# A four-layer graph network on one core: one program per graph stage replaced by streams that a planner interleaves, with sorting networks per block and half of their values in PSUM

## The chip, the cores and the metric

The kernel runs on one core of a Trainium2 chip. The metric is the device time of one execution in microseconds (us). The kernel before takes 6,414.04 us, the median of three runs (6,408.74 to 6,424.81).

A core has five engines that each run their own queue of instructions in order: TensorE (PE, matrix products and transposes; PEld is its weight load), VectorE (DVE), ScalarE (ACT), GpSimd (POOL) and SyncE (SP, which here only issues DMAs). Engines wait for each other through semaphores. The on-chip memories are SBUF and PSUM, both 128 partitions wide; TensorE writes its results to PSUM.

## The reference: what is computed

There are 16 graphs of 1,024 nodes with 64 channels each, a dense weighted adjacency matrix per graph (some 16 neighbours a node), and four pre-layernorm residual layers. Cut to what matters:

```python
h = relu(layernorm(x)); x = x + tanh([h, adj@h] @ W1 + b1) @ W2 + b2              # layer 0
h = relu(layernorm(x)); x = x + ((adj + I) @ h) / rowsum(adj + I)                 # layer 1
h = relu(layernorm(x)); x = x + mlp(h + quantiles(h over kept neighbours)) * mask # layer 2
h = relu(layernorm(x)); x = x + (adj @ h / colsum(adj)) @ Wn + h @ Ws + bias      # layer 3
```

Layer 2 is the irregular one. A node with more than 10 neighbours loses some of them, in both directions ("dilation": every `skip`-th by rank, `skip` from the count). For every node and channel the values of the kept neighbours are sorted, and the quantiles at 0.25, 0.5 and 0.75 are summed with the weights 0.25, 0.5, 0.25:

```python
sv = sort(where(valid, x_of_neighbour, big), axis=neighbours)
for tau, wt in zip((.25, .5, .75), (.25, .5, .25)):
    pos = tau * (m - 1); lo, hi = floor(pos), ceil(pos)
    agg += wt * (sv[lo] * (1 - (pos - lo)) + sv[hi] * (pos - lo))
```

## The kernel before

All work of interest is in `direct_path`. (`general_path` is a slower way that is run after it only where a node's neighbour count lies outside what the direct path provides for; with these inputs it is not run.) A graph's 1,024 nodes are 8 blocks of 128 partitions. A loop over `b` (at the end of the function) treats graph `b` up to its gathers, and in the same pass the sorting of graph `b-1`. The work of one graph is:

1. `load_graph` (L834): loads 8 row blocks of the adjacency, turns each with TensorE (L847), copies it back by ScalarE (L848) into `adjt`, writes the 0/1 neighbour mask `nb` on VectorE (L850, L852), counts neighbours, spills the turned matrix to DRAM (`adjt_d`, for layer 3), and sums degrees.
2. `dilated` (L869): ranks of neighbours by prefix matmuls (L892, L895), ScalarE's `Abs` (L899) and a compare on VectorE (`gone`, L900); then the kept neighbours as keys and their counts (L906 to L917).
3. `layer0` (L1052); then `order` (L923), which sorts the nodes by their kept count: `pos` is each node's place in that order (L938).
4. `neighbour_lists` (L941): the keys are scattered into sorted order through DRAM with 8 indirect DMAs (L946), loaded back block by block, and the neighbour numbers of each node are read out 8 at a time with VectorE's MAX8 (L960) and MATCH_REPLACE (L963). The indices of all blocks are made in one instruction (`index`, behind L967), then the quantile weights (L972 to L992).
5. `layer1` (L1066), the layernorm for layer 2 (`preln`, L791 on, with a memset on GpSimd, L806), and the store of its result `h_d` to DRAM (L1144).
6. Gathers and sorting: since the nodes are sorted by count, block 0 needs room for up to 38 neighbours and the last ones for 13. `GROUPS` lists (first block, blocks, most, least) for five groups. For each group, `aggregate` of the graph before runs on VectorE: a Batcher sorting network of `max` and `min` over whole 64-channel rows (L1031) that moves each value between two SBUF buffers (`raw`, `other`), the weights (L1044), a reduce (L1047), a store (L1048). Then `gather` (L1007) fetches this graph's neighbours: one indirect DMA of 128 rows by 64 channels for each block and place, 152 a graph, issued by GpSimd.
7. `layer2` (L1087) for the graph before: 8 indirect DMAs bring the sorted-order result back to node order (`res`, L1090), an add (L1092), transposes (L814), an MLP; then `layer3` (L1106), which reloads `adjt_d`, and the store of the output.

Order: the tile framework keeps each engine's instructions in about the order of the program text and inserts the waits. So on GpSimd's one queue lie, for each pass of the loop, the 8 scatters of graph `b`, its 152 gathers, and behind these the 8 read-backs of graph `b-1`. On TensorE's queue the transposes of `layer2` (L814) of graph `b-1`, which wait for those read-backs, lie ahead of the transposes of the adjacency (L847) of graph `b+1`. Each `raw` buffer exists once (`raws`, `bufs=1`), so a group's gathers of graph `b` follow its sorting of graph `b-1`.

Of the kernel before, what the change touches and what calls it, by code (L numbers as in the profile page):

```python
# [17 lines left out]
P = 128  # L18
# [14 lines left out]

GROUPS = [(0, 1, 38, 17), (1, 1, 20, 15), (2, 2, 18, 12), (4, 2, 16, 10), (6, 2, 13, 1)]
KW = N + 2

E_ID, E_ONE, E_CAP, E_LOW, E_CN, E_Q, E_END = 0, 128, 256, 264, 272, 280, 320
# [3 lines left out]
def _span(cap, low):  # L43

    return (low - 1) // 4, -(-3 * (cap - 1) // 4)


def _network(cap, low):


    n = 1
    while n < cap:
        n *= 2
    layers, a = [], 1
    while a < n:
        layers.append([(i, i + a) for i in range(n - a) if i // a % 2 == 0])
        a *= 2
    a, e = n // 4, 1
    while a > 0:
        d = e  # L60
        while d > 0:
            layers.append([(i, i + d * a) for i in range(a, n - d * a) if i // a % 2 == 1])
            d //= 2
        a, e = a // 2, 2 * e + 1
    lo, hi = _span(cap, low)
    live, kept = set(range(lo, hi + 1)), []
    for layer in reversed(layers):
        layer = [(i, j, i in live, j in live) for i, j in layer if j < cap and (i in live or j in live)]
        for i, j, _, _ in layer:
            live |= {i, j}  # L70
        if layer:
            kept.append(layer)
    return kept[::-1]


def _patterns(items):


    left, out = set(items), []
    while left:  # L80
        best = None
        for x in sorted(left):
            steps = sorted({(y[2] - x[2], y[3] - x[3]) for y in left if y[:2] == x[:2] and y > x})

            def run(start, v):
                row = [start]
                while (z := (*x[:2], row[-1][2] + v[0], row[-1][3] + v[1])) in left:
                    row.append(z)
                return row

            for v in [None, *steps]:
                row = [x] if v is None else run(x, v)
                if best is None or len(row) > len(best[0]):
                    best = (row, x, [(len(row), *(v or (0, 0)))])
                for w in steps if v else []:
                    cover, m = list(row), 1
                    while all((z := (*x[:2], r[2] + m * w[0], r[3] + m * w[1])) in left and z not in cover
                              for r in row):
                        cover += [(*x[:2], r[2] + m * w[0], r[3] + m * w[1]) for r in row]
                        m += 1  # L100
                    if m > 1 and len(cover) > len(best[0]):
                        best = (cover, x, [(m, *w), (len(row), *v)])
        left -= set(best[0])
        out.append(best[1:])
# [3 lines left out]
def _program(cap, low):  # L108


    home, out = [0] * cap, []
    for layer in _network(cap, low):
        for greater in (True, False):
            items = [(home[i], home[j], i, j) for i, j, a, b in layer if (a if greater else b)]
            out += [(greater, p) for p in _patterns(items)]
        for i, j, _, _ in layer:
            home[i] ^= 1
            home[j] ^= 1
    lo, hi = _span(cap, low)
    return out, _patterns([(home[q], 0, q, q - lo) for q in range(lo, hi + 1)])  # L120


QT = sum((_span(cap, low)[1] + 1 - _span(cap, low)[0]) * n for _, n, cap, low in GROUPS)
# [582 lines left out]

@with_exitstack
def direct_path(ctx: ExitStack, tc: tile.TileContext, t: dict, out: bass.AP, flag):


# [6 lines left out]
    loads = ctx.enter_context(tc.tile_pool(name="loads", bufs=2))  # L717
    graph = ctx.enter_context(tc.tile_pool(name="graph", bufs=1))
    nodes = ctx.enter_context(tc.tile_pool(name="nodes", bufs=2))
    lists = ctx.enter_context(tc.tile_pool(name="lists", bufs=2))  # L720
    work = ctx.enter_context(tc.tile_pool(name="work", bufs=2))
    raws = ctx.enter_context(tc.tile_pool(name="raws", bufs=1))
    psum = ctx.enter_context(tc.tile_pool(name="psum", bufs=1, space=bass.MemoryType.PSUM))
    dram = ctx.enter_context(tc.tile_pool(name="dram", bufs=2, space=bass.MemoryType.DRAM))

    def bank(dt=F32):
        return psum.tile([P, 2048 // mybir.dt.size(dt)], dt, tag="t", name="pt", bufs=4)

    def bank2():
        return psum.tile([P, N], F32, tag="t2", name="pt2", bufs=2)  # L730

    def big(shape, dt=F32):

        return work.tile(shape, dt, tag="big", name="big", bufs=3)

    def mid(shape, dt=F32):

        return work.tile(shape, dt, tag="mid", name="mid", bufs=4)

    tt, ts, act = nc.vector.tensor_tensor, nc.vector.tensor_scalar, nc.scalar.activation  # L740

# [15 lines left out]
    nc.vector.memset(bad, 0.0)  # L757

# [10 lines left out]
    def along(name, src):  # L769
        w = const.tile([P, C], F32, name=name)  # L770
        nc.gpsimd.dma_start(w, bass.AP(tensor=src.tensor, offset=src.offset, ap=[[0, P], [1, C]]))
        return w[:, None, :].to_broadcast([P, NB, C])

    w01, w02 = weight("L0_gnn_W1", 2 * C), weight("L0_gnn_W2", C)
    b01, b02 = column("L0_gnn_b1", C), along("b02", t["L0_gnn_b2"])
    w21, w22 = weight("L2_gnn_W1", C), weight("L2_gnn_W2", P)
    b21, b22 = column("L2_gnn_b1", P), along("b22", t["L2_gnn_b2"])
    w3n, w3s = weight("L3_gnn_W_neighbors", C), weight("L3_gnn_W_self", C)
    b3 = along("b3", t["L3_gnn_bias"])
# [5 lines left out]
    pm = bank()  # L785
    nc.tensor.transpose(pm[:, :B * NB], maskf, identf[:B * NB, :B * NB])
    mask = const.tile([P, B, NB], F32, name="mask")
    nc.vector.tensor_copy(mask.rearrange("p b i -> p (b i)"), pm[:, :B * NB])


    def preln(x):  # L791

        ha = nodes.tile([P, NB, C + 1], F32, name="ha", bufs=3)
        s = nodes.tile([P, 4, NB], F32, name="stat")
        xc = mid([P, NB, C])
        sq = mid([P, NB, C])
        nc.vector.tensor_reduce(s[:, 0], x, AX.X, ALU.add)
        ts(s[:, 1], s[:, 0], 1.0 / C, None, op0=ALU.mult)
        tt(xc, x, s[:, 1, :, None].to_broadcast([P, NB, C]), ALU.subtract)
        act(sq, xc, AF.Square)  # L800
        nc.vector.tensor_reduce(s[:, 2], sq, AX.X, ALU.add)
        act(s[:, 3], s[:, 2], AF.Sqrt, bias=eps, scale=1.0 / C)
        nc.vector.reciprocal(s[:, 2], s[:, 3])
        tt(xc, xc, s[:, 2, :, None].to_broadcast([P, NB, C]), ALU.mult)
        act(ha[:, :, :C], xc, AF.Relu)
        nc.gpsimd.memset(ha[:, :, C:], 1.0)  # L806
        return ha

    def transposed(h, dst):

        for q in range(2):
            p = bank()
            for u in range(4):
                nc.tensor.transpose(p[:C, u * P:(u + 1) * P], h[:, 4 * q + u, :C], identf)  # L814
            nc.scalar.copy(dst[:, q * 512:(q + 1) * 512], p[:C, :])  # L815

    def messages(h, rows_of, dst, p0, n=C):

        p = bank2()
        for j in range(NB):  # L820
            a = rows_of(j)
            for q in range(2):
                s = slice(q * 512, (q + 1) * 512)
                nc.tensor.matmul(p[p0:p0 + n, s], h[:, j, :n], a[:, s], start=j == 0, stop=j == NB - 1)  # L824
        nc.scalar.copy(dst, p[p0:p0 + n, :])

    def per_node(p, lhs, w):

        for i in range(NB):
            nc.tensor.matmul(p[:, i * C:(i + 1) * C], lhs[:, i * P:(i + 1) * P], w, start=True, stop=True)  # L830
# [3 lines left out]
    def load_graph(b):  # L834


        adjt = graph.tile([P, NB, N], F32, name="adjt")
        nb = graph.tile([P, NB, KW], F16, name="nb")
        mn = nodes.tile([P, NB], F32, name="mn")
        for i in range(NB):  # L840
            a = loads.tile([P, N], F32, name="a")
            nc.sync.dma_start(a, adj[b, i * P:(i + 1) * P, :])
            for q in range(2):
                p = bank()
                for u in range(4):
                    j = 4 * q + u
                    nc.tensor.transpose(p[:, u * P:(u + 1) * P], a[:, j * P:(j + 1) * P], identf)  # L847
                nc.scalar.copy(adjt[:, 4 * q:4 * q + 4, i * P:(i + 1) * P],  # L848
                               p.rearrange("p (u m) -> p u m", m=P))
            ts(nb[:, i, :N], a, 0.0, None, op0=ALU.is_gt)  # L850
            d = slice(i * P, (i + 1) * P)
            tt(nb[:, i, d], nb[:, i, d], offdiag, ALU.mult)  # L852
            sink = lists.tile([P, N], F16, name="sink", bufs=1)
            act(sink, nb[:, i, :N], AF.Copy, accum_out=mn[:, i:i + 1])
        adjt_d = dram.tile([NB, P, N], F32, name="adjt_d")
        deg = nodes.tile([P, 3, NB], F32, name="deg")
        for j in range(NB):
            nc.sync.dma_start(adjt_d[j], adjt[:, j])
            sink = lists.tile([P, N], F16, name="sink", bufs=1)
            act(sink, adjt[:, j], AF.Copy, accum_out=deg[:, 0, j:j + 1])  # L860
# [414 lines left out]
```

## Time and profile before

| what | value |
|---|---|
| median of three runs | 6,414.04 us (6,408.74 to 6,424.81) |
| span of the profiled execution | 6,913.4 us (7.8% above the median) |
| granted TensorE clock, mean | 0.625 |
| VectorE busy | 3,475.0 us, 50%, 8,634 instructions |
| GpSimd busy | 2,968.2 us, 43%, 2,770 instructions |
| TensorE busy | 2,119.5 us, 31%, 9,027 matmuls |
| ScalarE busy | 1,383.5 us, 20%, 2,178 instructions |
| gathers, L1007 | 2,432; 2,635.4 us, 1,084 ns each; 1,581.4 us of idle before them |
| sorting networks, L1031 (the two largest groups of the page) | 1,488 of 528 ns and 1,424 of 485 ns |
| longest kind of wait | TensorE at L814 for VectorE's L1092: 2,687.6 us in 16 waits |
| DMA | 372.80 MB, mean 54 GB/s |

How to read it: the page describes one execution under the hardware profiler. Its span is from the first instruction to the last and is the time to which durations of the page belong; the median is from runs without it. "Busy" is the share of the span in which an engine executes an instruction, and says nothing of what it waits for. A group's line gives how many, their total, the mean duration of one in ns, and the idle time of the engine just before them with what ended it. The rows of digits cut the span in 40 slices; each digit is the busy share of a slice in tenths.

### The profile page before, as it was taken

Reading aid. Unit: us, or ns where it says so; the run is one execution under the profiler, and the core shown is the slowest. Engines: PE = TensorE matmul, PEld = TensorE weight load, DVE = VectorE, ACT = ScalarE, POOL = GpSimd, SP = SyncE. Lnnn points to the kernel's source line nnn. Section 1 sums busy time; section 2 is a strip of 40 time slices with the busy share of each in tenths; the row PEclk is TensorE's granted clock in tenths of the full one; section 3 lists DMA queues with packets and bytes.
Section 4 is the critical chain, followed back from the end, with each engine's and each line's share of the span. In section 5 each row is a group of like instructions: output and inputs, shape, how many; then the busy total and the mean of one; then the engine's idle time right before and its main releaser. Section 6 shows DMA issues by size and latency. Waiting matters only on the chain.

```text
span 6913.4 us, 34033 instructions
## 1 busy us (share of the span) xinstructions
PE 2119.5 (31%) x9027; PEld 1036.5 (15%) x9027; DVE 3475.0 (50%) x8634; ACT 1383.5 (20%) x2178; POOL 2968.2 (43%) x2770
## 2 busy tenths in 40 slices
PE   6230251402624035140261404504046400624003
PEld 3010121201311012120130102202022100312001
DVE  3247371663715637066370655607556471833826
ACT  5110141300412013030141202203023300403000
POOL 0626417164071631716417172270722746153460
PEclk8565575755856557575585656757567655856556
DMA  3311213112241131312323123131233221232211
GB/s 116 53 24 25 61 65 67 51 23 57 89 76 26 24 70 61 56 57 24 69 95 59 29 21 87 57 47 57 21 87 95 37 36 23 87 67 49 37 21 49
DMA packets 234412, 372.80 MB, mean 54 GB/s; under 512 B 119104, under 2 KB 119296, under 8 KB 234208
## 3 DMA queue, kind: packets, MB, share of 16 engines
q0 software_dynamic: 92608, 117.94, 13.9%
q1 hardware_dynamic: 141456, 251.93, 11.0%
q8 instruction: 73, 1.20, 0.1%
q14 instruction: 131, 1.07, 0.1%
q10 hardware_dynamic: 144, 0.66, 0.0%
HBM read 257.00 MB, written 113.31 MB: 54 GB/s over the span
## 4 chain that ended last, share of the span: by engine, by line
issue 27%; DVE 17%; POOL 17%; another core or an unknown queue 13%; PE 13%; DMA 8%; ACT 3%; POOLq 0%; DVEq 0%; SPq 0%; ACTq 0%
POOL raw L1007 15%; PE pt L824 5%; DVE found L960 4%; DVE other L1031 3%; DVE raw L1031 3%; DVE rest L963 3%; DMA keys_d<-nb,pos 3%; DMA at<-adjt_d 3%; POOL keys_d L946 1%; DMA a<-in_adj_dram 1%; PE pt L830 1%; PE pt L895 1%; PE pt L847 1%; DMA raw<-h_d,index 1%
## 5 line engine op out<-in xcount | busy, mean ns | idle before, releaser
L1007 POOL DMA_INDIRECT raw<-h_d,index x2432 | 2635.4, 1084 | 1581.4 <-issue 732.0
L1031 DVE TENSOR_TENSOR other<-raw 128x128 f32<-128x128 f32 (+8 forms) x1488 | 759.8, 528 | 356.4 <-DMA raw<-h_d,index 287.5
L814 PE MATMUL pt<-ef,res 128*64 128x128 f32 x128 | 30.6, 420 | 2687.6 <-DVE res L1092 2687.6
L1031 DVE TENSOR_TENSOR raw<-other 128x256 f32<-128x256 f32 (+10 forms) x1424 | 669.1, 485 | 10.5 <-issue 3.5
L806 POOL MEMSET ha<- 128x8 f32 x64 | 8.6, 144 | 1444.5 <-PE pt L824 1402.5
L824 PE MATMUL pt<-adjt,ha 128*65 128x512 f32 (+1 forms) x1024 | 480.4, 630 | 231.5 <-issue 209.1
L1092 DVE TENSOR_TENSOR res<-res,ha 128x512 f32<-128x512 f32 x16 | 11.1, 691 | 1058.0 <-DMA res<-agg_d,pos 1058.0
L946 POOL DMA_INDIRECT keys_d<-nb,pos x128 | 194.4, 1519 | 687.9 <-DVE pos L938 431.8
L847 PE MATMUL pt<-ef,a 128*128 128x128 f32 x1024 | 234.5, 407 | 685.4 <-DMA a<-in_adj_dram 462.7
L815 ACT COPY big<-pt 64x512 f32<-64x512 f32 x96 | 55.3, 578 | 1877.2 <-PE pt L814 1460.1
L814 PEld LDWEIGHTS pt<-ef,res 128*64 128x64 f32 x128 | 19.9, 168 | 2694.0 <-DVE res L1092 2603.2
L895 PE MATMUL pt<-eh,nbt 128*128 128x512 f16 (+3 forms) x1536 | 339.9, 361 | 186.4 <-issue 122.0
L850 DVE TENSOR_SCALAR nb<-a 128x1024 f16<-128x1024 f32 x128 | 89.2, 697 | 481.5 <-DMA a<-in_adj_dram 339.4
L848 ACT COPY adjt<-pt 128x512 f32<-128x512 f32 x256 | 147.6, 585 | 826.0 <-remote 613.5
L900 DVE TENSOR_SCALAR gone<-ab,sf 128x1024 f16<-128x1024 f16 x128 | 61.5, 481 | 496.8 <-issue 258.1
L847 PEld LDWEIGHTS pt<-ef,a 128*128 128x128 f32 x1024 | 192.0, 214 | 727.2 <-issue 600.4
L824 PE MATMUL pt<-at,ha 128*64 128x512 f32 x512 | 264.1, 647 | 83.0 <-DMA at<-adjt_d 82.7
L960 DVE MAX8 found<-rest 128x8 f16<-128x1024 f16 x224 | 270.4, 1216 | 0.5
L899 ACT ACTIVATE ab<-pt,sf 128x1024 f16<-128x1024 f32 x128 | 142.8, 1116 | 512.4 <-remote 328.1
L895 PEld LDWEIGHTS <-nbt 128*128 128x128 f16 x1536 | 156.5, 106 | 508.5 <-issue 246.6
L824 PEld LDWEIGHTS pt<-adjt,ha 128*65 128x65 f32 (+1 forms) x1024 | 146.5, 146 | 550.4 <-issue 531.3
L1031 DVE TENSOR_TENSOR other<-raw,other 128x256 f32<-128x256 f32 (+4 forms) x592 | 205.1, 348 | 33.2 <-remote 24.5
(138 smaller groups left out, 4763.3 us busy)
## 6 DMA issues: line engine op xcount, KB each, us to landing
a<-in_adj_dram SPq DMA_DIRECT2D x128, 512.0 KB
adjt_d<-adjt SPq DMA_DIRECT2D x128, 512.0 KB
at<-adjt_d SPq DMA_DIRECT2D x128, 512.0 KB
raw<-h_d,index POOLq DMA_INDIRECT x2432
k<-keys_d SPq DMA_DIRECT2D x128, 256.5 KB
x<-in_x_dram SPq DMA_DIRECT2D x16, 256.0 KB
h_d<-ha SPq DMA_DIRECT2D x16, 256.0 KB
out_dram<-x SPq DMA_DIRECT2D x16, 256.0 KB
```

Source lines behind the costliest of these rows:

```text
L824: nc.tensor.matmul(p[p0:p0 + n, s], h[:, j, :n], a[:, s], start=j == 0, stop=j == NB - 1)
L830: nc.tensor.matmul(p[:, i * C:(i + 1) * C], lhs[:, i * P:(i + 1) * P], w, start=True, stop=True)
L847: nc.tensor.transpose(p[:, u * P:(u + 1) * P], a[:, j * P:(j + 1) * P], identf)
L848: nc.scalar.copy(adjt[:, 4 * q:4 * q + 4, i * P:(i + 1) * P], p.rearrange("p (u m) -> p u m", m=P))
L850: ts(nb[:, i, :N], a, 0.0, None, op0=ALU.is_gt)
L895: nc.tensor.matmul(p[:, o:q * 512 + 512], nbt[:, j, :], stair[:, o - j * P:q * 512 + 512 - j * P], start=False, stop=j == 4 * q + 3)
L899: act(ab, p, AF.Abs, bias=sf[:, 2, i:i + 1], scale=2.0)
L946: nc.gpsimd.indirect_dma_start(keys_d, bass.IndirectOffsetOnAxis(ap=pos[:, i:i + 1], axis=0), nb[:, i, :], None)
L960: nc.vector.max(out=e, in_=src)
L963: nc.vector.match_replace(out=rest, in_to_replace=e, in_values=src, imm_value=0.0)
L1007: nc.gpsimd.indirect_dma_start(raw[:, s, i * C:(i + 1) * C], None, h_d, bass.IndirectOffsetOnAxis(ap=index[:, at:at + 1], axis=0))
L1031: tt(o, a, b, ALU.max if greater else ALU.min)
```

## The change

It rewrites `direct_path`; the general path and the host side stay, but for tables.

- **Order.** The loop over graphs is gone. The work of a graph is some fifteen generators ("streams"): `tail` (layers 2 and 3), `load_a`, `load_x`, two of `turn` (transposes), `masks`, two of `ranks`, two of `keyed`, `ordered`, `fetched`, `listed`, `weighted`, `layers01`, `spill`, `gathered`, `sorted_`. Each yields operations with an engine, a cost in us, and the regions that they read and write. A planner, when the program is built, takes again and again the operation that can start first, and among those that can start within 0.02 us the one of the lowest rank: `10*b` and a small number for preparation and tail of graph `b`, `10*b+1000` for its gathers and networks. That fixes each engine's order; the framework's own scheduling is turned off. Buffers are allocated once and streams wait in the planner until one is free; PSUM is three pairs of banks for matmuls and one pair (`places`, 16 slots of 64 channels) for the networks.
- **Blocks.** Each of the 8 blocks has a network of its own, with the caps and least counts `CAPS` and `LOWS`: 132 gathers a graph, where there were 152. Only the places that some quantile needs are kept (`_needed`). Five `raw` buffers serve the 8 blocks: blocks 5, 6 and 7 use those of blocks 1, 2 and 3. The index is written block by block.
- **Networks.** Of the values that a layer of the network writes, one side goes to PSUM and one to SBUF as the table `SIDES` says; `_boxes` joins operations with up to three strides. Instructions of the networks: 5,248 before, 6,384 after.
- **To ScalarE and TensorE.** Layernorm's centering and squares are 8 ScalarE instructions with an accumulator, its scaling 8 more with bias and scale; column sums of the adjacency come from the accumulator of the copies behind the transposes; biases and residual adds become matmuls; the weighted places are summed by matmuls with the identity (1,120 in all) where VectorE reduced them; aggregates are stored by block (128 DMAs for 80).

The core of the diff; the new functions that it calls, `_boxes` and `_program` (the list of a network's operations and where each value lies), follow from the description above:

```diff
-GROUPS = [(0, 1, 38, 17), (1, 1, 20, 15), (2, 2, 18, 12), (4, 2, 16, 10), (6, 2, 13, 1)]
+CAPS = (33, 19, 17, 15, 14, 13, 11, 10)
+LOWS = (19, 17, 15, 14, 13, 11, 10, 3)
+PLACES = 16
...
+class _Planner:
+    def start(self, op):
+        t = self.free.get(op.engine, 0.0)
+        for aps, writes in ((op.ins, False), (op.outs, True)):
+            for name, lo, hi in aps:
+                for a, b, end, wrote, engine in self.used.get(name, ()):
+                    if a < hi and lo < b and (writes or wrote):
+                        if engine != op.engine:
+                            end += 0.12 + (0.4 if op.engine == "DVE" and wrote else 0.0)
+                        t = max(t, end)
+        return t
...
+    def run(self):
...
+            heads = {}
+            for s in self.streams:
+                if s[3] is not None:
+                    heads.setdefault(s[3].engine, []).append((self.start(s[3]), s))
+            best = None
+            for these in heads.values():
+                first = min(t for t, _ in these)
+                t, s = min(((t, s) for t, s in these if t <= first + 0.02), key=lambda c: (c[1][0], c[1][1]))
+                if best is None or t < best[0]:
+                    best = (t, s)
...
+            self.commit(op, t)
...
-    def aggregate(g, raw, wts, agg_d):
...
-            tt(o, a, b, ALU.max if greater else ALU.min)
...
-        nc.vector.tensor_reduce(agg, part.rearrange("p q w -> p w q"), AX.X, ALU.add)
...
+    def tt(o, a, b, op):
+        return _Op("DVE", 0.068 + n_of(o) / 960, lambda: nc.vector.tensor_tensor(o, a, b, op), [o], [a, b])
...
+    def gather(o, src, at):
+        return _Op("POOL", 1.25, lambda: nc.gpsimd.indirect_dma_start(
+            o, None, src, bass.IndirectOffsetOnAxis(ap=at, axis=0)), [o], [src, at], 1.8)
...
+    def preln(x, h, s):
...
+        for i in range(NB):
+            yield act(junk, x[:, i], AF.Square, bias=s[:, 1, i:i + 1], accum=s[:, 2, i:i + 1])
+        yield act(s[:, 3], s[:, 2], AF.Sqrt, bias=eps, scale=1.0 / C, table="sqrt")
...
+        for i in range(NB):
+            yield act(h[:, i, :C], x[:, i], AF.Relu, bias=s[:, 4, i:i + 1], scale=s[:, 2, i:i + 1])
...
+    def listed(b):
...
+            yield ts(index[:, c], found[:, c], -1.0, ALU.mult, float(N), ALU.add)
+            post(("index", b, k))
...
+    def gathered(b):
+        yield "wait", ("h", b)
+        index, h_d = indexes[b % 2], h_ds[b % 3]
+        for k in range(NB):
+            yield "wait", ("index", b, k)
+            before = [(c, i) for c in (b - 1, b) for i in range(NB) if home[i] == home[k] and (c, i) < (b, k)]
+            if before and before[-1][0] >= 0:
+                yield "wait", ("block", *before[-1])
+            raw = raws[home[k]]
+            for s in range(CAPS[k]):
+                at = LOFF[k] + s
+                yield gather(raw[:, s, :], h_d, index[:, at:at + 1])
+            post(("raw", b, k))
...
+    def sorted_(b):
...
+                mem = (raws[home[k]], other, places)
...
+                yield tt(o, a, c, ALU.max if kind == "max" else ALU.min)
...
+            def issue(p=p, n=n):
+                for q in range(n):
+                    nc.tensor.matmul(p, identf, part[:, q, :], start=q == 0, stop=q == n - 1)
+            yield pe(0.12 * n, issue, [p], [part[:, :n]])
+            yield copy(aggs[:, k], p)
...
+            yield dma(agg_ds[b % 2][k * P:(k + 1) * P], aggs[:, k])
...
-    for b in range(B + 1):
...
+    for b in range(B):
+        plan.add(10 * b, tail(b))
...
+        plan.add(10 * b + 2, ordered(b))
+        plan.add(10 * b + 4, listed(b))
+        plan.add(10 * b + 3, layers01(b))
...
+        plan.add(10 * b + 1000, gathered(b))
+        plan.add(10 * b + 1000, sorted_(b))
+    with tc.manual_schedule():
+        plan.run()
```

## The prediction

> **What bounds the kernel now.** I read the page's first two sections, then the chain, then the waits, then the timeline of one graph's gathers.
>
> ```profile
> span 6913.4 us, 34033 instructions
> DVE  3247371663715637066370655607556471833826
> POOL 0626417164071631716417172270722746153460
> issue 27%; DVE 17%; POOL 17%; another core or an unknown queue 13%; PE 13%; DMA 8%; ACT 3%; POOLq 0%; DVEq 0%; SPq 0%; ACTq 0%
> L1007 POOL DMA_INDIRECT raw<-h_d,index x2432 | 2635.4, 1084 | 1581.4 <-issue 732.0
> ```
>
> No engine bounds it: DVE is busy 50%, POOL 43%, TensorE 31%, and the rows of tenths swing with a period of two to three slices, one graph. The chain hands from engine to engine. First gather at 193 us, end of the last at 6,707: (6,707−193)/16 = 407 us a graph. Its 152 gathers take 152×(1.084+0.305 gap, from the "issue" wait) = 211 us; for 196 us POOL gathers nothing. Why the next graph's preparation does not run beside the gathers, the waits tell (us in total, times, longest):
>
> ```profile
> PE pt L814 <- DVE res L1092: 2687.6, 16, 310.2
> ACT big L815 <- PE pt L814: 1460.1, 50, 234.4
> POOL raw L1007 <- DVE s L972: 519.4, 10, 53.1
> POOL keys_d L946 <- DVE pos L938: 431.8, 15, 102.4
> ```
>
> TensorE stands 168 us a graph in front of the transposes of layer 2, which need the result read back through POOL's queue, behind all 152 gathers; the next graph's TensorE work is queued behind them. POOL then waits for that preparation.
>
> **The change part by part.** All costs are in the profiled execution's time; it is 6,913/6,414 = 1.078 of the median (range of the runs 6,409 to 6,425).
>
> *Gathers and POOL.* 152 gathers a graph become 132: indirect DMAs 16×(132+8 scatters+8 read-backs) = 2,368 for 2,688. An undisturbed one and its gap, from the timeline:
>
> ```profile
> 3140.83 9.22 POOL L1007 DMA_INDIRECT raw<-h_d,index  x1 [0.31 <-issue]
> 3149.13 2.71 DVE L1047 TENSOR_REDUCE agg<-part 128x128 f32<-128x1536 f32 x1
> 3150.35 0.94 POOL L1007 DMA_INDIRECT raw<-h_d,index  x1 [0.30 <-issue]
> ```
>
> 0.944+0.305 = 1.249 us; 2,368× = 2,958 us. The 9.22 is a gather held while DVE ran networks; it ends 0.92 after the reduce began. I set all gathers against what DVE ran: 1,860 with idle DVE mean 0.943; 360 begun under two-SBUF-input network operations 1.706 (+0.76); 28 under the compare of L850 1.787 (+0.84); 26 under the reduce 0.944. After, of 3,600 us or so, DVE does such two-SBUF work for 381 us (1,600 operations; the other 5,664 have an input in PSUM) and compares for 128 us: 10.6% of 2,368 is 251×0.76 = 191 us, 3.6% is 84×0.84 = 71. MAX8 and MATCH_REPLACE (631 us) never met a gather: bounds 0 (like the reduce) and 17.5%×2,368×0.84 = 350; I take 0, being one-input like the reduce, and keep 350. Head: the index is written per block, so gathers need not wait for a graph's whole lists (668/16 = 42 us) and start at about 193−42+4 = 155; tail from the last read-back (6,844.6 to the end 6,913, 69) about 75. POOL's side: 2,958+191+71+155+75 = 3,450.
>
> The Trainium skill, "SBUF — State Buffer", section "Who interferes with whom", says a DVE instruction with at most one SBUF input outside the two-port modes leaves GpSimd alone, and one with two SBUF inputs contends only with SBUF reads. The trace agrees with 0.944 under the reduce and 1.706 under two inputs. By that rule the operations with an input in PSUM cost nothing, as taken.
>
> The smaller caps hold these inputs exactly (their largest and smallest kept counts, block by block, are the new lists), so the general path stays unrun.
>
> *DVE.* Start to start, an SBUF tensor_tensor costs 0.068+n/960 (n elements a row). By that: networks 5,248 operations, 1,852 us, become 6,384, 1,590 (smaller caps; one block at a time and three places for a value, so more and smaller ones); weights 168→98; the sum over kept places 115→0 (to TensorE, 1,120 identity matmuls, about 0.3 each from L830's 0.276: 336 us); lists 668→631; layernorms 160→60 and layer adds 134→56 (to ScalarE's bias and accumulate forms and to bias matmuls). Sum of all instructions: 3,352→2,677.
>
> But dependence costs. An operation that needs the one just before it starts later:
>
> ```profile
> 3476.62 1.21 DVE L1031 TENSOR_TENSOR other<-raw 128x1024 f32<-128x1024 f32 x1
> 3477.86 1.23 DVE L1031 TENSOR_TENSOR raw<-other 128x1024 f32<-128x1024 f32 x1
> 3479.00 0.48 DVE L900 TENSOR_SCALAR gone<-ab,sf 128x1024 f16<-128x1024 f16 x1
> ```
>
> The dependent one starts 1.24 after its predecessor, the independent one 1.14: over 219 pairs 0.116 more. The before program has 420 immediate dependences of 8,412; the after 5,036 of 9,038, for it plans one block's network at a time: 584 us for 49. DVE's occupied time: 2,677+584 = 3,261 for 3,401. With 115 idle at the head and the tail's 75: 3,451.
>
> Writes to PSUM (3,088) are not in the trace of before. Reads are, at no cost: 687 ns against 683 for the same shape:
>
> ```profile
> L1064 DVE TENSOR_TENSOR x<-x,pt 128x512 f32<-128x512 f32 x16 | 11.0, 687 | 206.4 <-PE pt L830 191.2 <-remote 15.2
> L799 DVE TENSOR_TENSOR mid<-x,stat 128x512 f32<-128x512 f32 x64 | 43.6, 683 | 0.3
> ```
>
> Bounds −0.068 (the fixed part vanishes: −210 us) to +0.116 each (+358); I take 0, by the read. The Trainium skill, "Perfetto Trace Analysis", section "Optimizing Scalar/DVE Operations", puts DVE's overhead at about 60 ns on SBUF and 125 on PSUM; an estimate by it, 65 ns on 5,664, adds 368 us of engine time. The reads of this trace (4 ns) do not show it.
>
> *ScalarE, TensorE, SP.* 512 squares and 512 Relus of 64 elements, 256 accumulator reads (0.2 each), copies: from 1,384 to some 1,730 us; TensorE 2,120 plus 336 and 124 for bias and residual matmuls, 2,580. Both lie beside POOL and DVE with over 800 us of idle left; without that cover, 350 and 460. SP issues 694 DMAs for 646 (aggregates by block, 128 for 80), waits apart a few us, hidden too.
>
> *Order and waits.* Build-time list scheduling puts read-backs and scatters between gathers (about two gathers, 2.5 us, from one to the next) and the next graph's preparation between network operations: the 196 us without gathers and TensorE's 2,688 go. What is late next: blocks 5 to 7 reuse raw buffers 1 to 3, so their gathers, and scatters queued behind them, wait for those sorts; three blocks of gathers (46×1.25 = 57 us) are the slack. TensorE's three bank pairs and in-order queues remain, with an order made from fixed costs.
>
> *Sum.* POOL 3,450, DVE 3,451: two equal bounds on different queues, each feeding the other, do not both run full. The nearest stretch where networks and gathers ran together:
>
> ```profile
> 3140.00:3160.00 20.00, 0.00 (x0) 0.00 (x0) 20.00 (x43) 2.54 (x6) 18.17 (x7) 0.50 0.06 13
> 3160.00:3180.00 20.00, 0.00 (x0) 0.00 (x0) 19.93 (x53) 1.15 (x2) 17.24 (x10) 0.50 0.08 18
> 3180.00:3200.00 20.00, 0.00 (x0) 0.00 (x0) 15.12 (x48) 0.00 (x0) 16.25 (x12) 0.50 0.24 22
> ```
>
> DVE (third pair of columns) is filled 55.05 of 60 = 92%. 3,450/0.92 = 3,750 profiled. The excess of 7.8% may be spread over everything (×0.928) or lie in gaps that vanish here (×1.0); midway 0.965: 3,620 us.
>
> **Rivals.**
> R1, a write to PSUM holds the next operation like a dependence: +358, (3,451+358)/0.92×0.965 = 4,000. Against: the reads cost nothing. For: half of all operations are of a kind never run here.
> R2, gathers are held by any DVE work, PSUM operands or not: 2,368×0.9×0.76 = 1,620 for the 262 counted: POOL 4,812, ×0.965 = 4,640. For: the 9.22 us gather outlived several instructions. Against: 0.944 under the reduce.
> R3, slower: overlap fails, as a TensorE or ScalarE instruction of one stream that waits for POOL again stands ahead of the next graph's preparation. Period 407−20×1.39+33 (535 us of new dependence, per graph) = 412; 16×412+193+206 (before's head and tail) = 6,991, ×0.928 = 6,490. It decides when under 5 us of the 196 a graph is hidden. For: PE in order, three bank pairs. Against: read-backs now stand between gathers.
> R4, no coupling loss and the profile's excess spread: 3,450×0.928 = 3,200. For: after 3,260 POOL gathered undisturbed (15.12 of 20 busy with its gaps, full); against: both bounds equal.
>
> ```profile
> 3260.00:3280.00 20.00, 0.00 (x0) 0.00 (x0) 0.00 (x0) 0.00 (x0) 15.12 (x17) 0.50 0.12 26
> ```
>
> **How the numbers follow.** Forecast 0.60 (own range 3,300 to 3,900: fill 85 to 98%, factor 0.928 to 1.0), R1 0.14, R4 0.13, R2 0.08, R3 0.05. The range 3,180 to 4,250 holds the forecast, R4 and R1 with some of the 350 for the lists; it leaves R2, R3 and tails, under 0.2. A change within 0.3% is about what a measurement of this kernel cannot tell from none. Faster 0.94 (all but R3, less the border's 0.01), same 0.01, slower 0.05.
>
> **What the changed kernel's profile would show.** First gather near 155 us, mean gather about 1.05 with 0.305 gaps, POOL and DVE both busy with no swing by graph, no wait of 100 us at the transposes of the read-back. If PSUM writes cost, 64-wide network operations stand over 0.135 apart where independent; if ports hold gathers, their mean goes to 1.7. Wrong above all if DVE's planned order waits: long idle stretches of DVE ahead of network operations for gathers, while POOL waits for DVE.

## The result and the profile after

The changed kernel takes 4,184.75 us (median of four runs, 4,181.67 to 4,189.4) against 6,419.43 us of the kernel before on the same chip: a ratio of 0.651, 95% interval 0.6493 to 0.6526. It is clearly faster, and 565 us slower than the forecast of 3,620: inside the range of 3,180 to 4,250, outside the forecast's own 3,300 to 3,900.

In the last two sets of runs the kernel before itself took 6,953 and 6,963 us instead of 6,399 to 6,436 (its profile in the first part spans 6,913), so runs of those two sets are compared only with runs of the same set, and runs of the other sets by their ratios to the kernel before.

The page of the changed kernel (engines' busy time, their tenths in 40 slices, the chain that ended last, the gathers' group):

```profile
span 4185.4 us, 43000 instructions
PE 2714.1 (65%) x12067; PEld 1439.6 (34%) x12067; DVE 3164.4 (76%) x9244; ACT 1655.9 (40%) x3858; POOL 2290.5 (55%) x2387
...
DVE  1478597878878788697877889677886978788582
...
POOL 0356446464574746647464664746467374647670
...
DVE 35%; PE 33%; DMA 11%; ACT 11%; issue 5%; POOL 4%; SPq 0%; DVEq 0%; ACTq 0%; POOLq 0%
...
L1095 POOL DMA_INDIRECT raw<-h_d,index x2112 | 2025.9, 959 | 877.1 <-issue 535.9
```

VectorE went from 50% to 76% busy and, between the head and the end, no longer falls below 5; GpSimd's row has lost its slices of 0, 1 and 2 there. From the start of one graph's gathers to the next are now 247 us in the middle of the run, where the first profile had 421 on average, 302 to 494. (The prediction's 407 runs from the first gather to the end of the last, divided by 16; counted so, it is now 244.) A gather takes 959 ns for 1,084. The span equals the unprofiled median this time.

But neither VectorE nor GpSimd is full. The waits (us in total, times, longest) say where the two stand:

```profile
POOL res L1095 <- PE pair L1283: 376.1, 18, 44.0
POOL keys_d L1099 <- DVE pos L1067: 155.0, 4, 94.5
...
POOL res L1095 <- DMA agg_d<-aggs: 91.7, 4, 38.5
...
DVE m L1339 <- DMA kt<-keys_d: 145.6, 20, 16.0
DVE gone L1067 <- ACT half L1082: 103.4, 57, 6.5
DVE den L1075 <- PE pair L1429: 98.8, 16, 15.2
```

GpSimd stops 38 to 48 us in front of the read-backs of ten graphs, less at the others (509 us in all, 32 a graph). L1283 is only the last event that the view could name; the timeline shows what they wait for (start, duration, engine, instruction, idle time before it):

```profile
2000.63 0.15 DVE L1339 CAST m<-kt 128x1 f32<-128x1 f16 x1 [11.21 <-DMA kt<-keys_d]
...
2002.62 0.95 POOL L1095 DMA_INDIRECT raw<-h_d,index  x1 [0.30 <-issue]
...
2016.57 0.69 DVE L1067 TENSOR_SCALAR nb<-a 128x1024 f16<-128x1024 f32 x1
...
2041.50 0.28 DVE L1061 TENSOR_TENSOR part<-raw,wts 128x128 f32<-128x128 f32 x1
...
2041.84 2.00 PE L1506 MATMUL pair<-part,ef 128*128 128x64 f32 x16 [0.62 <-DVE part L1061]
2043.88 0.21 ACT L1085 COPY aggs<-pair 128x64 f32<-128x64 f32 x1 [1.50 <-PE pair L1506]
...
2044.11 0.33 SPq L1089 DMA_DIRECT2D agg_d<-aggs  x1
...
2046.41 1.07 POOL L1095 DMA_INDIRECT res<-agg_d,pos  x1 [42.85 <-PE pair L1283]
```

The last gather ends at 2003.6. The read-back needs the last block's aggregate, which VectorE finishes at 2041.8, because its queue has 11 us of waiting for a key load, the next graph's lists to 2016.6 and its masks ahead of those networks. Behind the read-backs on GpSimd's queue stand the next gathers. The windows view of this stretch and of the one after it (columns: length; busy us and instructions of PE, PEld, DVE, ACT, POOL; granted clock, DMA share, GB/s):

```profile
2003.60:2046.40 42.80, 26.45 (x151) 15.55 (x151) 40.03 (x129) 17.96 (x34) 0.00 (x0) 0.70 0.45 167
2046.40:2238.00 191.60, 139.26 (x620) 71.51 (x619) 152.30 (x443) 88.82 (x218) 132.85 (x137) 0.79 0.35 80
```

In the first VectorE is busy 40 of 43 us and GpSimd does nothing; in the second VectorE is busy 152 of 192 us. So GpSimd waits for VectorE. VectorE hardly waits for the gathers: sorted by what ended them, its waits over 0.3 us are 404 us for ScalarE, 243 for TensorE, 146 for the key loads, which stand behind GpSimd's scatters, and 11 for gathers.

For the experiments two sums are taken from the traces: VectorE's idle time in gaps over 0.3 us (831 us here, with 128 before the first gather and 67 behind the last read-backs; the rest of the span, 3,354 us, is called occupied), and GpSimd's idle time before its indirect DMAs beyond the usual 0.305 us gap (read-backs 509, scatters 267 besides the first one's 95, gathers 234).

### The profile page after: what moved, and what is told of

Its sections match the earlier page's. It is cut to its first block, busy times and chain, and to the rows that moved or that the text cites. A ratio compares the mean times of both kernels' runs of the same rounds, so it can differ in the third digit from the quotient of the medians.

```text
span 4185.4 us, 43000 instructions
## 1 busy us (share of the span) xinstructions
PE 2714.1 (65%) x12067; PEld 1439.6 (34%) x12067; DVE 3164.4 (76%) x9244; ACT 1655.9 (40%) x3858; POOL 2290.5 (55%) x2387
## 4 chain that ended last, share of the span: by engine, by line
DVE 35%; PE 33%; DMA 11%; ACT 11%; issue 5%; POOL 4%; SPq 0%; DVEq 0%; ACTq 0%; POOLq 0%
PE pair L1137 13%; DVE places L1061 10%; DVE other L1061 6%; DVE found L1344 5%; DVE raw L1061 5%; PE pair L1256 5%; DMA kt<-keys_d 4%; PE pair L1506 4%; POOL raw L1095 4%; DVE rest L1346 3%; ACT junk L1082 3%; PE pair L1148 3%; ACT half L1082 2%; DMA at<-adjt_d 2%; DMA raw<-h_d,index 2%
## 5 line engine op out<-in xcount | busy, mean ns | idle before, releaser
L1095 POOL DMA_INDIRECT raw<-h_d,index x2112 | 2025.9, 959 | 877.1 <-issue 535.9
L1137 PE MATMUL pair<-adjt,h 128*65 128x512 f32 (+1 forms) x1024 | 487.3, 636 | 132.3 <-ACT h L1082 131.3
L1506 PE MATMUL pair<-part,ef 128*128 128x64 f32 x2240 | 336.1, 315 | 245.0 <-DVE part L1061 239.5
L1256 PE MATMUL pair<-eh,nbt 128*128 128x512 f16 (+3 forms) x1536 | 365.7, 384 | 151.5 <-ACT nbt L1244 151.5
L1095 POOL DMA_INDIRECT res<-agg_d,pos x128 | 123.0, 961 | 548.0 <-PE pair L1283 376.1
L1506 PEld LDWEIGHTS pair<-part,ef 128*128 128x128 f32 x2240 | 319.8, 228 | 291.2 <-DVE part L1061 160.3
L1137 PE MATMUL pair<-at,h 128*64 128x512 f32 x512 | 302.5, 734 | 101.9 <-DMA at<-adjt_d 90.5
L1061 DVE TENSOR_TENSOR raw<-other,places 128x128 f32<-128x128 f32 (+7 forms) x880 | 290.7, 346 | 20.6
L1061 DVE TENSOR_TENSOR places<-other,places 128x128 f32<-128x128 f32 (+7 forms) x800 | 284.3, 355 | 20.9
L1061 DVE TENSOR_TENSOR other<-raw,places 128x128 f32<-128x128 f32 (+5 forms) x896 | 264.5, 318 | 16.8
L1061 DVE TENSOR_TENSOR places<-raw,places 128x128 f32<-128x128 f32 (+4 forms) x784 | 238.9, 305 | 16.0
```

What stands on the lines that cost most here:

```text
L1061: return _Op("DVE", 0.068 + n_of(o) / 960, lambda: nc.vector.tensor_tensor(o, a, b, op), [o], [a, b])
L1095: return _Op("POOL", 1.25, lambda: nc.gpsimd.indirect_dma_start(o, None, src, bass.IndirectOffsetOnAxis(ap=at, axis=0)), [o], [src, at], 1.8)
L1256: nc.tensor.matmul(p[:, o:q * 512 + 512], nbt[:, j, :], stair[:, o - j * P:q * 512 + 512 - j * P], start=False, stop=j == 4 * q + 3)
L1506: nc.tensor.matmul(p, identf, part[:, q, :], start=q == 0, stop=q == n - 1)
```

## The experiments

**The planner's costs.** The fixed order comes from a cost for each operation. VectorE's leave out the gap between dependent operations; TensorE's add up to 1,879 us where the trace has it busy for 2,714. First the gap was told to the planner, then both.

```diff
                         if engine != op.engine:
                             end += 0.12 + (0.4 if op.engine == "DVE" and wrote else 0.0)
+                        elif wrote and op.engine == "DVE" and end == self.free["DVE"]:
+                            end += 0.116
```

> The planner is told that a VectorE operation that reads what the one just before it wrote starts 0.116 us later; nothing else is changed. Theory A (the fixed order is wrong, because it was made with VectorE costs that leave out this gap; POOL therefore stands 40 us a graph before the read-backs): 3,550 to 3,850 us, POOL's waits before the read-backs fall from 509 us to under 250, and fewer operations follow their producer directly. Rival B (VectorE's own occupied time with the chains through ScalarE and TensorE sets the period, whatever the order): 4,050 to 4,200 us, the waits stay. Rival C (TensorE's costs in the planner are what is wrong): within 2% of 4,185 us here, and under 3,900 us only where TensorE's costs are mended too.

Measured: 4,136 us, ratio 0.6422 (0.6396 to 0.6448), 1.4% less than the change. Instructions that wait for the one just before them fell from 5,036 to 3,818 in the program; VectorE's occupied time fell by 137 us to 3,217. But its idle time rose by 104 to 935, and GpSimd's waits moved from the read-backs (509 to 326) to gathers that wait for a raw buffer (234 to 485). Theory A falls on the time; B's time is met, though the waits did not stay, and C's for this run is met too.

```diff
-        return _Op("PE", cost, issue, outs, ins)
+        return _Op("PE", 1.45 * cost, issue, outs, ins)
```

> As the run with the dependence gap in the planner, and TensorE's costs in the planner times 1.45 (2,714 us busy in the trace for 1,879 in the planner). Theory A: within 2% of the run without the TensorE part. Rival B: 4,050 to 4,200 us. Rival C: at least 5% faster than the run without the TensorE part, under 3,900 us.

Measured: 3,940 us, ratio 0.6118 (0.6092 to 0.6143), 4.7% below the run without this line on the same chip. This is nearest to rival C (a little short of its 5% and its 3,900), and the fastest version that was measured beside a kernel before of 6,400. VectorE's occupied time stayed (3,201); its idle time fell by 197 to 738, most of it (325 to 150 us) in waits that TensorE ended. The waits of this kernel:

```profile
POOL raw L1097 <- DVE raw L1063: 423.0, 42, 36.1
...
POOL res L1097 <- DMA agg_d<-aggs: 82.2, 10, 34.1
...
DVE gone L1069 <- ACT half L1084: 271.0, 89, 10.0
```

The stop in front of the read-backs is nearly gone (89 us in all). What is left is gathers that wait for a sort to free its buffer, and VectorE waiting for chains through TensorE and ScalarE, the rank chain above all (ScalarE ends 504 us of VectorE's waits).

TensorE's costs alone:

> TensorE's costs in the planner times 1.45, VectorE's as in the changed kernel. If TensorE's costs are what misled the planner, most of the 250 us that both corrections won together are here: 3,920 to 4,000 us. If they act only together with the dependence gap: 4,050 to 4,200 us.

Measured: 5,523 us beside a kernel before of 6,953, ratio 0.7949 (0.7905 to 0.7993). Neither expectation can be read from it; whether TensorE's costs alone bring the gain stays open.

**Networks all in SBUF.** One part of the change undone, in the changed kernel's own planner:

```diff
-SIDES = ((2, 0, 0, 0, 1, ...), ...)
-FINALS = ("stay", "stay", "stay", "stay", "stay", "S", "S", "S")
+SIDES = tuple((2,) * n for n in (21, 15, 15, 10, 10, 10, 10, 10))
+FINALS = ("S",) * 8
```

> All values of the networks in SBUF, order planned as in the changed kernel; VectorE issues 784 more instructions, an estimate of 53 us (0.068 each) to 144 us (0.184, each dependent). If an operand in PSUM neither costs nor saves: 4,200 to 4,330 us, and the mean gather stays at 0.95 to 1.0. If operations with two SBUF inputs hold gathers as in the kernel before (0.76 us more for those that meet one): mean gather 1.15 to 1.35, and 4,300 to 4,900 us. If writing to PSUM is what held VectorE: 3,850 to 4,100 us.

Measured: 4,119 us, ratio 0.6399 (0.6366 to 0.6432): 1.7% faster than the change, and between the expectations, 19 us above the third. Its page:

```profile
PE 2649.6 (64%) x12067; PEld 1405.3 (34%) x12067; DVE 2960.5 (72%) x10028; ACT 1656.4 (40%) x3858; POOL 2525.2 (61%) x2387
...
L1086 POOL DMA_INDIRECT raw<-h_d,index x2112 | 2217.8, 1050 | 892.8 <-issue 554.0
```

Both sides of the trade are seen. Gathers are held: 1,050 ns for 959, over all indirect DMAs 1.063 for 0.963 us, 0.1 x 2,368 = 237 us of GpSimd. VectorE has 784 instructions more and yet is occupied for 3,048 us, 306 less. The reason is in the changed kernel's timeline of VectorE:

```profile
2036.28 0.29 DVE L1061 TENSOR_TENSOR raw<-places,other 128x128 f32<-128x128 f32 x1
2036.49 0.29 DVE L1061 TENSOR_TENSOR places<-places,other 128x128 f32<-128x128 f32 x1
2036.81 0.29 DVE L1061 TENSOR_TENSOR raw<-other,places 128x128 f32<-128x128 f32 x1
2037.02 0.29 DVE L1061 TENSOR_TENSOR places<-other,places 128x128 f32<-128x128 f32 x1
```

The second operation reads nothing that the first wrote and starts 0.21 us after it. The third reads `places`, which the second has just written to PSUM, and starts 0.32 us after it, though all four have the same size. In the SBUF version only 1,993 instructions wait for the one just before them, against 5,036: between networks' operations within SBUF the program mostly has no such wait, after a write to PSUM it mostly has one (after 2,724 of 3,088 in the trace). The sizes fit: 3,043 waits fewer at 0.12 us are 365 us, less 53 for 784 instructions more at 0.068, 312 us. Of the 306 us saved on VectorE, 229 came back as longer idle time (831 to 1,060), so that the whole gain is 70 us.

**Relieving one engine at a time, the order kept.** In each of these the planner still counts the work that is left out, so every queue keeps its order.

```diff
-                yield gather(raw[:, s, :], h_d, index[:, at:at + 1])
+                got = gather(raw[:, s, :], h_d, index[:, at:at + 1])
+                if s % 4 == 3:
+                    got.issue = lambda: None
+                yield got
```

> Every fourth place of a block is not gathered (32 to 28 gathers of each graph are left out, so the output is not the reference's); the order of everything else is the planned one, for the planner still counts 1.25 us for each. If VectorE's order holds POOL (theories A and B): 4,050 to 4,200 us, and POOL waits longer. If POOL's time is what bounds the period: 16 x 30 x 1.265 = 607 us less, 3,550 to 3,700 us.

Measured: 4,104 us, ratio 0.6366 (0.6337 to 0.6396). 464 DMAs, 587 us of GpSimd's time, bring 0.0144 x 6,435 = 93 us, as theories A and B had it. GpSimd only waits longer, as this line of its waits shows against 376.1 and 44.0:

```profile
POOL res L1097 <- PE pair L1285: 466.1, 18, 66.5
```

VectorE, by the MATCH_REPLACE instructions (each MAX8 then reads the loaded keys again):

```diff
-                yield _Op("DVE", 1.135, lambda e=e, src=src: nc.vector.max(out=e, in_=src), [e], [src])
+                yield _Op("DVE", 1.135, lambda e=e, kt=kt: nc.vector.max(out=e, in_=kt[:, :N]), [e], [src])
...
-                    yield _Op("DVE", 1.2, lambda e=e, src=src: nc.vector.match_replace(
-                        out=rest, in_to_replace=e, in_values=src, imm_value=0.0), [rest], [e, src])
+                    yield _Op("DVE", 1.2, lambda: None, [rest], [e, src])
```

> VectorE relieved, order kept: the 208 MATCH_REPLACE are left out (each later MAX8 finds the first eight again, so the lists and the output are wrong), the planner still counts them. 208 x 1.33 = 277 us of VectorE's 3,164. Theory D (VectorE's occupied time is in the loop that sets the period): at least 80% comes back, 3,900 to 3,960 us. Theory E (no engine bounds the period; the order of each queue was fixed with TensorE's costs far too low, and the chains through TensorE set it): less than half, 4,050 to 4,185 us.

Measured: 4,010 us, ratio 0.626 (0.6244 to 0.6275). VectorE is busy 282 us less (277 were counted); that brings 0.025 x 6,399 = 160 us, 57%: between the two theories.

TensorE, by the message products:

```diff
+            if j not in (0, NB - 1):
+                issue = lambda: None
             yield pe(1.27, issue, [p], [h[:, j], a])
```

> TensorE relieved, order kept: of the eight row blocks that the message products of layers 0, 1 and 3 sum over, six are left out (the output is wrong), the planner still counts them. 6/8 of 487 + 303 = 592 us of TensorE's 2,714. Theory E: more than half comes back, 3,600 to 3,880 us. Theory D: less than a quarter, 4,040 to 4,185 us.

Measured: 4,076 us, ratio 0.6372 (0.6361 to 0.6383): 0.0138 x 6,399 = 88 us. Theory E falls and D's time is met: TensorE's time by itself is not what sets the period. The busy time of this run and the products of layer 3, first in the changed kernel and then here, show that the relief was smaller than counted:

```profile
PE 2283.1 (56%) x10915; PEld 1338.3 (33%) x10915; DVE 3164.8 (78%) x9244; ACT 1655.6 (41%) x3858; POOL 2288.7 (56%) x2387
...
L1137 PE MATMUL pair<-at,h 128*64 128x512 f32 x512 | 302.5, 734 | 101.9 <-DMA at<-adjt_d 90.5
...
L1137 PE MATMUL pair<-at,h 128*64 128x512 f32 x128 | 113.1, 1037 | 103.6 <-DMA at<-adjt_d 92.2 <-ACT big L1085 11.4
```

TensorE is busy 431 us less, not 592: the mean granted clock fell from 0.742 to 0.675, and one such product takes 1,037 ns where it took 734. Sorted by the clock granted while they ran, 345 of the changed kernel's 512 products ran at the full clock (0.60 us) and 130 at half of it (1.07 us); of the 128 left here, 113 ran at half.

ScalarE, by the squares:

```diff
-            yield act(junk, x[:, i], AF.Square, bias=s[:, 1, i:i + 1], accum=s[:, 2, i:i + 1])
+            got = act(junk, x[:, i], AF.Square, bias=s[:, 1, i:i + 1], accum=s[:, 2, i:i + 1])
+            if i not in (0, NB - 1):
+                got.issue = lambda: None
+            yield got
```

> ScalarE relieved, order kept: of the eight squares with an accumulator of each layernorm six are left out (the output is wrong), the planner still counts them. 6/8 of 178 + 96 = 205 us of ScalarE's 1,656. Theory E: a quarter to a half, since the layernorms lie in the chains, 4,080 to 4,140 us. Theory D: none, 4,150 to 4,200 us.

Measured: 4,111 us, ratio 0.6425 (0.6414 to 0.6436): 0.0085 x 6,399 = 54 us, in the range of theory E. ScalarE is busy 167 us less, not 205, so a third came back.

| relieved | by (us of its time) | came back (us) | share |
|---|---|---|---|
| GpSimd | 587 | 93 | 16% |
| VectorE | 282 | 160 | 57% |
| TensorE | 431 | 88 | 20% |
| ScalarE | 167 | 54 | 32% |

By the intervals of the ratios the times that came back are sure to some 13 to 22 us. No engine returns its time in full, and each returns some. VectorE weighs most. The period is a round of waits through all four queues, not one engine's load.

**The blocks alone, in the kernel before.**

```diff
-GROUPS = [(0, 1, 38, 17), (1, 1, 20, 15), (2, 2, 18, 12), (4, 2, 16, 10), (6, 2, 13, 1)]
+GROUPS = [(0, 1, 33, 19), (1, 1, 19, 17), (2, 1, 17, 15), (3, 1, 15, 14), (4, 1, 14, 13), (5, 1, 13, 11),
+          (6, 1, 11, 10), (7, 1, 10, 3)]
```

> The kernel before with the eight blocks' own caps and networks, as one part of the change alone (the loop, its order and SBUF networks stay): 320 gathers fewer at 1.39 us, 445 us; the networks grow from 5,248 instructions of 1,852 us to 7,152 of 1,658 us. If the gathers stand alone on the path as the prediction counts them: 6,420 - 0.93 x 445 = 6,000 us, 5,950 to 6,100. If the sorting stands ahead of the gathers instead, the smaller instructions give some back: 6,100 to 6,400 us.

Measured: 5,704 us, ratio 0.8917 (0.8902 to 0.8932), 696 us less than the kernel before, more than either expectation. 320 gathers at 1.39 are 445 of it, the networks' smaller sum at most 195 more. The rest was not tested; that eight raw buffers come free one by one where five did would be one reason. The wait that holds TensorE is still there:

```profile
PE pt L815 <- DVE res L1093: 2146.0, 16, 260.8
```

**The overlap alone undone, in the changed kernel.**

```diff
             k = (b * NB + i - 4)
+            if b:
+                yield "wait", ("gathered", b - 1)
```

> The changed kernel with one wait more in the planner: the load of a graph's adjacency, and with it the whole preparation, comes after all gathers of the graph before. If the 196 us a graph without gathers that now lie beside the gathers are what the change won: the period rises from 248 us by 100 to 150, 5,600 to 6,500 us. If the smaller networks, the moved work and the finer blocks won most of it: under 5,000 us.

Measured: 7,270 us beside a kernel before of 6,953, ratio 1.0466 (1.0387 to 1.0545), more than either expectation: slower than the kernel before, and 32% slower than the run of the same set with TensorE's costs mended (5,523). From graph to graph 451 us, 207 with gathers and 244 without; GpSimd's row of tenths swings as before:

```profile
span 7260.4 us, 42892 instructions
...
POOL 1514205142151421504215052150522505224052
```

Blocks, moved work and PSUM are all in this kernel, and sorting still runs beside gathers, as it does in the kernel before. Without preparation beside the gathers they win nothing. But this edit takes away more than the change had added: in the kernel before some preparation did run beside gathers (in the first profile all 64 transposes of one adjacency, L847, lie within the gathers from 2,766 to 2,959 us). And the changed kernel itself was not measured in this set. So the run shows that the gain needs the overlap, not how many us the overlap is worth.

**Networks in SBUF with TensorE's costs mended.** Both edits above, twice.

> Networks all in SBUF and TensorE's costs in the planner times 1.45, no dependence gap in the planner. If the two gains (about 70 and 200 to 250 us) come from different waits they add: 3,800 to 3,900 us, a version faster than both kernels. If the gathers that SBUF operands hold (1.06 us each) are now on the path: 3,930 to 4,050 us.

> The kernel with networks in SBUF and TensorE's costs in the planner times 1.45 once more, because in its first set of runs the kernel before took 6,953 us. Beside a kernel before at about 6,400 us: if TensorE's costs alone are what misled the planner, the gain of some 200 us shows without the dependence gap as well, and with the 70 us of SBUF networks the ratio is 0.59 to 0.61, 3,780 to 3,920 us. If the two corrections act only together: 0.63 to 0.65, as with SBUF networks alone.

Measured: 5,304 and 5,296 us beside kernels before of 6,953 and 6,963, ratio 0.7629 both times (0.7582 to 0.7677 and 0.7579 to 0.7679). Against the run of the same set with TensorE's costs mended and half of the values in PSUM (5,523) it is 4.0% faster, so that SBUF networks win there too. The two expectations cannot be told apart from these runs. Whether it beats 3,940 us could not be seen.

## Why the prediction was right or wrong

**Overlap: right.** TensorE's 2,688 us in front of the read-back's transposes are gone, and of the 196 us a graph without gathers 63 us of GpSimd's waits and 20 us of read-backs and scatters are left; in the run without preparation beside the gathers all of the gain is lost. R3 did not happen; the longest TensorE wait on VectorE's network results is 50.3 us, at L1506.

**Gathers and POOL: right in kind, too high.** 2,368 x (0.963 + 0.305) = 3,003 us where 2,958 + 191 + 71 = 3,220 was forecast. The gathers held by VectorE cost 0.019 x 2,368 = 46 us, not 262: the two-SBUF operations left are few and short (0.24 us each by the prediction's count), and the 219 gathers begun under one took 1.05 us. Bound 0 for the lists was right: 211 gathers under MAX8 took 0.945 us, 131 under MATCH_REPLACE 0.944. The first gather came at 168 us (forecast 155), the tail took 66 (75). R2 (whose sum is 4,808, not 4,812) falls: gathers are held by two SBUF inputs and by the mask and rank compares (35 begun under a `nb` compare took 1.20 us), not by any VectorE work. The Trainium skill, "SBUF — State Buffer", section "Who interferes with whom", says that a VectorE instruction with two SBUF inputs contends with a GpSimd instruction that reads SBUF, and that one with at most one SBUF input, outside the two-port modes, does not. The traces agree: indirect DMAs took 1.063 us with the networks all in SBUF and 0.963 with half of their values in PSUM.

**DVE: nearly right.** Occupied 3,354 us where 3,261 was forecast; a wait behind a PSUM write measured 0.128 us where 0.116 was taken. Independent operations behind a write to PSUM start 0.005 us later than their size says (226 pairs), those behind a write to SBUF 0.003 (2,017 pairs), so R1's extra price does not exist. The price of PSUM was in the sum already, as the 5,036 dependences; what the prediction did not see is that most of them come from PSUM itself and not from planning one block at a time: 3,043 go when the networks lie in SBUF. The Trainium skill, "Perfetto Trace Analysis", section "Optimizing Scalar/DVE Operations", puts VectorE's overhead at about 60 ns on SBUF and 125 on PSUM, 65 more, 368 us by the prediction's estimate; the SBUF version saves (306 + 784 x 0.068)/5,664 = 63 ns. In size that agrees; in the trace it lies between dependent operations alone.

**ScalarE, TensorE, SP: busy times right, "hidden" wrong.** 1,656 us for 1,730, 2,714 for 2,580, the sums' matmuls 336 for 336. But calling them hidden by 800 us of idle time was wrong: relieved of some work, these two engines gave back a fifth and a third of it, costs that were wrong for TensorE in the planner cost 197 us of idle time on VectorE, and 647 of VectorE's 831 us of idle time end with TensorE or ScalarE.

**Sum: this is the step that failed, with its factor.** The fill of 92% (the share of the time in which the fuller engine is occupied) was taken from a stretch in which only networks and gathers ran. With the preparation among them VectorE's side, 3,354 + 115 + 75 = 3,544 us, fills 85% of 4,185; at 92% it would be 3,852, so 333 us of the miss are the fill. The mended planner gets 250 us by filling gaps and cutting waits; what the rest of VectorE's 738 us of idle time there would need stays open.

The factor 0.965 is the second miss, 3,750 - 3,620 = 130 us. The span of the changed kernel's profile is its median, and what lengthened the first profile was idle time, no share of every duration: VectorE, ScalarE and TensorE stood there 3,420 us, added over the three, in waits whose end the trace cannot name, as in this line of its waits:

```profile
ACT adjt L848 <- remote: 613.5, 54, 47.0
```

In the profile of the kernel before with the blocks alone, whose span is within 9 us of its median, such waits are 16 us, and MAX8 takes 1,216 ns and an undisturbed gather 0.944 us as in the first profile. The third miss is VectorE's own 93 us, 101 at a fill of 92%. The three add up to 564 of the 565 us.

Each of the two sizes came out at an end of the prediction's own bands (85 to 98%, 0.928 to 1.0). Both together give 3,450/0.85 = 4,059, more than the 3,900 that its own range allowed. That 4,185 lies below 4,250 is luck: the room above 3,900 was made for R1 and for the 350 us of the lists, and neither took place. R4, full coupling, falls with the fill.

The prediction's last sentence, that a planned order could leave VectorE and GpSimd waiting for each other, is half of what the trace shows. GpSimd does wait for VectorE; VectorE waits for gathers for only 11 us. The partner that the prediction left out is the chain through TensorE and ScalarE, which it had called hidden.

## What to carry to other kernels

Where several in-order queues share the work, two engines at the same sum do not give that sum: take the fill from a stretch in which every queue that hands over is active; here it was 85%, not 92%. An order fixed at build time is only as good as its costs; here correcting two of them, each by one line, won another 6%. Moving an operand to PSUM to keep a neighbour's port free also buys a wait behind every write that is read next; count both, by undoing the one part.

## What the runs showed of the hardware beyond expectation

- A VectorE operation that reads what the one before wrote to PSUM starts 0.128 us later than its size says, and behind a write to SBUF, where the program waits, 0.117. In the program with half of the networks' values in PSUM 5,036 of 9,038 instructions wait so, with all in SBUF 1,993 of 9,822.
- Taking matmuls away lowered TensorE's mean granted clock from 0.742 to 0.675: 113 of 128 products that were left ran at half of the full clock, where 130 of 512 had, and their mean went from 734 to 1,037 ns.
- MAX8 and MATCH_REPLACE (one SBUF input) never lengthened an indirect DMA: 0.945 and 0.944 us against 0.946 beside an idle VectorE.
